# Attention in a two-layer block: outputs moved behind the exponentials, one more buffer, LN(x) in pairs, small tiles shared

## The chip, the core and the metric

The kernel runs on one core of one Trainium2 chip. The core has five engines with a queue of instructions each: TensorE (PE in the profile; PEld are its weight loads), VectorE (DVE), ScalarE (ACT), GpSimd (POOL) and SyncE (SP), and 16 DMA engines that they share. An engine works through its queue in order, and waits where an instruction waits. The metric is the device time of one execution in microseconds (us); lower is better.

## The reference

The input x is 4 images of 32 x 32 tokens with 384 channels, in float32. Two layers follow, each an attention part and a feed-forward part with a residual:

```python
x = x + L0_conv(LN(x))      # attention with 12 heads of 32, described below
x = x + L0_ffn(LN(x))       # 4 experts of width 1536, each token goes to 2 of them
x = x + L1_conv(LN(x))      # outlook attention over 3x3 neighbourhoods
x = x + L1_ffn(LN(x))       # a feed-forward part whose weights are Kronecker products
```

The change lies in the first of these:

```python
attn = softmax(q @ k.T * scale)               # per image and head: 1024 x 1024
gidx = argmax(q @ gp.T)                       # each query goes to one of 48 groups
q_mean = mean of q over each group
tidx = top_k(q_mean @ k.T, 96)                # per group: its 96 best keys
col = number of groups that have chosen a key
attn = attn * (row * col)                     # row is 1 for each query
attn = attn / (attn.sum(axis=queries) + 1e-8) # normalized again, per key
out = (attn @ v) @ proj_w.T
```

## The kernel before

The program runs attention for the four images, then the experts, then the second layer. Everything in the first layer is emitted in an order written out by hand: within `tc.manual_schedule`, the queues of PE, DVE, ACT and SP get their instructions in the order of the Python code (only POOL's are ordered by the framework). What stands earlier in the code runs earlier on its engine.

**Steps.** `attention` has 48 heads (4 images x 12), and each head has 4 steps (`PAIRS`), so 192 steps. Keys lie on the partitions: a step handles two blocks of 128 keys against all 1024 queries. The loop at L838 emits each step in this order:

- `out` (L680), for the step seven earlier (`OUT`): four products of the weighted values `wv` with the two tiles `e` of that step, summed over a head's four steps in the PSUM tile `ps_o`. After a head's last one `keep` (L685) copies `ps_o` to the SBUF tile `po`, and four DMAs put it into the head's rows of `q`: two from SP, then two from POOL that accumulate.
- `scores` (L606): four products of 32 rows each, k times q, into two PSUM tiles `ps_s` of 128 x 1024 (there are two).
- At a head's first step, `gather` (L641) for the head before: ScalarE copies the PSUM sums `z` to `zr`, which go by DMA through a row in DRAM into `zz`.
- `exps` (L619): two `exp` on ScalarE, `ps_s` to two tiles `e`. `ep` has `EBUFS` = 14 of these.
- `spread` (L653), in the second step: adds the halves of `zz` into `zall`, takes reciprocals, and sends them by DMA to all partitions (`rz`).
- Other work: projections of the image before, values, and the units of `prepared` (L785). The generators `groups` and `prepare` yield a unit with its estimated TensorE time and a condition; units are taken while `spent` is below `goal`, which grows by `PACE` = 2.6 us a step.
- `total` (L636): four products of ones with the new tiles `e`, into `ps_z`.
- `share` (L664), for the step six earlier (`SHARE`): VectorE multiplies two tiles `e` by `rz` and the factor `inv`, sums them, and scales the values into `wv`.
- `search` (L795), twice: up to two running searches for the 96 best keys take one turn each, a pass of ScalarE over 128 x 1024 (`Sign` with a sum, written to `junk`, which lies in `below`) or a few small VectorE instructions.

**LN(x).** `prepare` (L442) normalizes an image's eight token tiles one by one: a unit of 0.9 us emits a tile's normalization on ScalarE (`xn`, two buffers), and then the three TensorE transposes and the ScalarE copy of the tile before (`turn`). Several units can fall into one step.

**Small tiles.** `zall` holds the sums of all 48 heads; at the end (L886 to L898) they are checked for their range together with other conditions. The router (`Router.route`, L1255, and after it `first` and `schedule`) sorts tokens to experts, with temporaries named by `temp`; its table is written by 16 indirect DMAs for each image from POOL's queue.

Of the kernel before, what the change touches and what calls it, by code (L numbers as in the profile page):

```python
# [10 lines left out]
FP = mybir.dt.float32  # L11
AF = mybir.ActivationFunctionType
ALU = mybir.AluOpType
AX = mybir.AxisListType
PSUM = bass.MemoryType.PSUM

P = 128
# [21 lines left out]
AHEAD = 3  # L39
EBUFS = 14  # L40
REACH = 2 * IMG + 2
# [112 lines left out]
def attention(net, outer, router, x, x1, unsafe, qkv_wT, gpT, proj_wT, proj_w, gate_w, gate_b):  # L154
# [24 lines left out]
    with ExitStack() as ctx:  # L179
# [72 lines left out]
        junk = below.bitcast(mybir.dt.bfloat16)  # L252
        zall = const.tile([P, NHEAD, NB], FP, name="zall")
        onehot = const.tile([P, B * KC * NB // 2], FP, name="onehot")
# [187 lines left out]
        def prepare(b):  # L442
# [10 lines left out]
            im["mean"] = few.tile([P, NB], FP, name="mean", tag="mean", bufs=3)  # L453
            im["std"] = few.tile([P, NB], FP, name="std", tag="std", bufs=3)
            im["x"] = few.tile([P, NB, NE], FP, name="gate_x", tag="gate_x", bufs=3)

            def turn(xn, o):
                ps = psum()
                for c in range(KC):
                    nc.tensor.transpose(ps[:, c * P : (c + 1) * P], xn[:, c * P : (c + 1) * P], net.ident)  # L460
                nc.scalar.copy(xnT[:, :, o : o + P], ps[:, :C].rearrange("p (c t) -> p c t", c=KC))

            behind = None
            for half in range(2):
                if half and b:
                    yield 0, after(2)
                xt = xts.pop((b, half))
                mv = tiny.tile([P, 4, 2], FP, name="ln_mv", tag="ln_mv", bufs=2)
                rs = tiny.tile([P, 4], FP, name="ln_rs", tag="ln_rs", bufs=2)
                off = tiny.tile([P, 4], FP, name="ln_off", tag="ln_off", bufs=2)  # L470
                for t in range(4):
                    st = tiny.tile([P, 6], FP, name="ln_st", tag="ln_st", bufs=2)
                    nc.vector.bn_stats(st, xt[:, t, :])
                    nc.vector.bn_aggr(mv[:, t, :], st)
                    if t % 2:
                        yield 0.3, None
                std = im["std"][:, 4 * half : 4 * half + 4]
                nc.scalar.activation(std, mv[:, :, 1], AF.Sqrt, bias=net.eps["c"])
                yield 0.3, after(1) if b else None
                nc.vector.tensor_copy(im["mean"][:, 4 * half : 4 * half + 4], mv[:, :, 0])  # L480
                nc.vector.reciprocal(rs, std)
                nc.vector.scalar_tensor_tensor(off, mv[:, :, 0], -1.0, rs, ALU.mult, ALU.mult)
                for t in range(4):
                    yield 0.9, None
                    xn = work.tile([P, C], FP, name="xn", tag="xn")
                    nc.scalar.activation(
                        xn, xt[:, t, :], AF.Identity, bias=off[:, t : t + 1], scale=rs[:, t : t + 1]
                    )
                    if behind is not None:
                        turn(*behind)  # L490
                    behind = xn, (4 * half + t) * P
                if half == 0 and b:
                    fetch(b, 1)
                elif half and b + 1 < B:
                    if b == 0:
                        gating()
                    fetch(b + 1, 0)
            yield 0.9, None
            turn(*behind)
            for c in range(KC):  # L500
# [83 lines left out]
        class Head:  # L584
# [68 lines left out]
            def spread(self):  # L653

                z = zall[:, self.n, :]
                nc.vector.tensor_tensor(z, self.zz[:, 0, :], self.zz[:, 1, :], ALU.add)
                rr = tiny.tile([P, NB], FP, name="rr", tag="rr", bufs=2)
                nc.vector.reciprocal(rr, z)
                there = rows.tile([NTOK], FP, name="r_row", tag="r_row")
                nc.sync.dma_start(out=there.rearrange("(p i) -> p i", i=NB), in_=rr)  # L660
                self.rz = work.tile([P, NTOK], FP, name="rz", tag="rz")
                nc.sync.dma_start(out=self.rz, in_=there.partition_broadcast(P))

            def share(self, u):  # L664
# [20 lines left out]
            def keep(self):  # L685

                po = work.tile([P, 512], FP, name="po", tag="po", bufs=1)
                nc.scalar.copy(po, self.po)
# [30 lines left out]
        def project(b, t):  # L719
            im = images[b]  # L720
            r = b * NTOK + t * P
            if t == 0:
                im["o"] = few.tile([P, NB, NE], FP, name="gate_o", tag="gate_o")
                im["mv"] = few.tile([P, NB, 2], FP, name="mv", tag="mv")
# [21 lines left out]
        def routed(b):  # L746
# [11 lines left out]
            nc.scalar.activation(rs, im["mv"][:, :, 1], AF.Sqrt, bias=net.eps["t"])  # L758
            logit = few.tile(wide, FP, name="logit", tag="logit")
            part = few.tile(wide, FP, name="logit_part", tag="logit_part")  # L760
            mean = im["mean"]
# [76 lines left out]
        for step in range(STEPS + OUT + 2):  # L838
            n, u = divmod(step, PAIRS)
            if 0 <= step - OUT < STEPS:  # L840
                heads[(step - OUT) // PAIRS].out((step - OUT) % PAIRS)
                if (step - OUT) % PAIRS == PAIRS - 1:
                    heads[(step - OUT) // PAIRS].keep()
            if n < NHEAD:
# [3 lines left out]
            if n < NHEAD:  # L848
                heads[n].exps()
            b, i = divmod(step, PAIRS * NH)  # L850
            goal = min(goal + (RAMP if step < 12 else PACE), spent + MOST)
# [33 lines left out]

        good = ep.tile([P, NTOK], FP, name="good", tag="e")[:, : 2 * NHEAD * NB + B * KC * NB // 2 + 2 * B * 5]  # L886
        nz = NHEAD * NB
        flat = zall.rearrange("p n i -> p (n i)")
        nc.vector.tensor_scalar(good[:, :nz], flat, ZMAX, None, ALU.is_le)
        nc.vector.tensor_scalar(good[:, nz : 2 * nz], flat, 1 / ZMAX, None, ALU.is_ge)  # L890
        no = 2 * nz + B * KC * NB // 2
        nc.vector.tensor_scalar(good[:, 2 * nz : no], onehot, 8.0, None, ALU.is_equal)
        nc.vector.tensor_scalar(good[:, no : no + B * 5], topped[:, 0, :], 0.0, None, ALU.is_gt)
# [292 lines left out]
class Router:  # L1186
# [68 lines left out]
    def route(self, b, logit, mean, rs):  # L1255
# [39 lines left out]

        run = [self.temp(f"run_{n}", wide) for n in range(2)]
        src, d = sel, 1
# [32 lines left out]
        yield  # L1330
        ids = self.temp("ids", [P, NB, self.LINE], mybir.dt.int32)
        nc.gpsimd.iota(ids, pattern=[[P, NB], [0, self.LINE]], base=b * NTOK, channel_multiplier=1)
# [13 lines left out]
    def first(self):  # L1346
# [4 lines left out]
        nc.vector.tensor_scalar(full, self.upto[:, B - 1, :], -float(XB), None, ALU.add)  # L1351
        fills = self.temp("fills", shape)
        nc.vector.tensor_tensor(
# [54 lines left out]
    def schedule(self, pool):  # L1408

        nc = self.nc  # L1410
        shape = [P, NE, self.NJ]
        fills = self.temp("fills", shape)
        taken = self.temp("taken", [P, NE])
# [798 lines left out]
```

## Time and profile before

| what | value |
|---|---|
| median of 3 runs | 2989.33 us (2986.28 to 2994.61) |
| the profiled execution | 2999.3 us, span 2997.0 us |
| attention | start to about 1290 us |
| mean granted TensorE clock | 0.97 |
| scores, sums, outputs (L612, L630): instructions each | 1536 |
| one `exp` (L622) | 1109 ns, 384 times |
| one `share` multiplication (L668) | 1272 ns, 384 times |
| one `Sign` pass (L366) | 1149 ns, 160 times |

A line of the profile names the code line, the engine, the operation, and what it writes and reads (`ps_z<-e,rt_ones` is a product of `e` and ones into `ps_z`), then a count. In the waits, a line tells who waited for whom: total, times and the longest. In an order of time, a line has start, length, and in brackets the idle time of the engine before it and what ended it. In a stretch of time, a line has the stretch, its length, and then busy time and instructions of PE, PEld, DVE, ACT and POOL, then the granted TensorE clock, the busy share of the DMA engines and GB/s. Each float32 product shows as two instructions.

### The profile page before, as it was taken

What the parts mean: (1) busy time and instruction counts of PE and PEld (TensorE: products, weight loads), DVE (VectorE), ACT (ScalarE), POOL (GpSimd) and SP (SyncE); (2) the same over time, 40 slices, a digit from 0 to 9 for tenths busy, and PEclk for the clock granted to TensorE, in tenths of its full rate; (3) what the DMA queues carried; (4) which work ended last, traced back from release to release, by engine and by line L of the source; (5) the groups of instructions that cost most, each with busy time, mean ns of one, the idle gap of its engine ahead of it and who ended that gap; (6) DMA issues with size and microseconds to landing.
All of it is one profiled execution on the core that took longest, in us unless ns stands there. A gap on an engine that the chain in (4) does not pass through costs nothing.

```text
span 2997.0 us, 36619 instructions
## 1 busy us (share of the span) xinstructions
PE 2793.7 (93%) x13236; PEld 1509.3 (50%) x13236; DVE 1349.4 (45%) x3703; ACT 1217.0 (41%) x2023; POOL 399.3 (13%) x499
## 2 busy tenths in 40 slices
PE   6979998999899987688999999999999998999988
PEld 4323333333333431156777777777777754444433
DVE  1466676766776677534000001111111137877642
ACT  3777777677777765312111211211211122222125
POOL 1000000200021003113111112222221101100000
PEclk9999999999999998889999999999999999999989
DMA  5133334322322233254445545555555617654432
GB/s 100 46 87 99 92 92 117 81 56 62 96 57 57 65 93 104 69 172 153 182 166 189 190 175 194 213 214 196 206 214 201 232 52 231 197 173 145 161 103 86
DMA packets 216991, 405.90 MB, mean 135 GB/s; under 512 B 83505, under 2 KB 177905, under 8 KB 203745
## 3 DMA queue, kind: packets, MB, share of 16 engines
q1 hardware_dynamic: 186656, 190.77, 21.5%
q0 software_dynamic: 27152, 209.66, 20.4%
q10 hardware_dynamic: 2992, 3.03, 0.3%
q8 instruction: 107, 1.75, 0.3%
q14 instruction: 84, 0.68, 0.1%
HBM read 305.35 MB, written 49.99 MB: 119 GB/s over the span
## 4 chain that ended last, share of the span: by engine, by line
PE 50%; DMA 3%; issue 3%; DVE 3%; ACT 1%; POOL 0%; DVEq 0%; POOLq 0%; ACTq 0%; SPq 0%
PE ps_h L1584 18%; PE ps_y L1601 17%; PE ps_a L1712 4%; PE ps_y L1814 3%; DMA yt<-yg,index 2%; PE ps_wo L1830 1%; PE ps_v L1756 1%; PE ps_h L1984 1%; PE ps_c L1777 1%; PE ps_y L1995 1%; PE ps_t L1541 1%; PE ps_z L630 1%; DMA o<-in_x_dram 1%; PE ps_o L2008 0%; PE ps_o L630 0%
## 5 line engine op out<-in xcount | busy, mean ns | idle before, releaser
L1588 ACT ACTIVATE h<-ps_h,up 128x256 f32<-128x256 f32 x420 | 198.6, 473 | 930.2 <-PE ps_h L1584 930.2
L1584 PE MATMUL ps_h<-xbT,up 128*128 128x256 f32 x2520 | 557.1, 382 | 0.8 <-DVE xbT L1542 0.7
L1601 PE MATMUL ps_y<-down,h 128*128 128x384 f32 x1680 | 556.9, 489 | 0.0
L1584 PEld LDWEIGHTS ps_h<-xbT,up 128*128 128x128 f32 x2520 | 482.7, 192 | 77.0 <-DVE xbT L1542 1.1
L668 DVE CUSTOM_DVE_ANT_0 e<-e,rz,inv 128x1024 f32<-128x1024 f32 x384 | 474.2, 1272 | 59.5 <-DMA rz<-r_row 59.3
L622 ACT ACTIVATE e<-ps_s,shift 128x1024 f32<-128x1024 f32 x384 | 406.5, 1109 | 199.6 <-PE ps_s L612 199.2
L1601 PEld LDWEIGHTS ps_y<-down,h 128*128 128x128 f32 x1680 | 318.5, 191 | 208.2 <-issue 3.5
L1606 DVE TENSOR_TENSOR y<-ps_y,down 128x384 f32<-128x384 f32 x70 | 39.0, 558 | 729.6 <-PE ps_y L1601 729.6
L630 PE MATMUL ps_z<-e,rt_ones 128*32 128x512 f32 x1536 | 297.4, 636 | 63.1 <-ACT e L622 63.1
L630 PE MATMUL ps_o<-e,wv 128*32 128x512 f32 x1536 | 277.6, 644 | 25.7 <-DVE wv L675 15.0
L612 PE MATMUL ps_s<-q,k 32*128 32x512 f32 x1536 | 224.1, 654 | 0.0
L695 POOL DMA_DIRECT2D q<-po x96 | 75.7, 876 | 1063.1 <-DMA q<-po 547.1
L366 ACT ACTIVATE below<-tk_left,tk_bound 128x1024 bf16<-128x1024 f32 (+1 forms) x160 | 183.9, 1149 | 11.3 <-DVE tk_bound L372 7.0
L1712 PE MATMUL ps_a<-wa,xnT 128*128 128x486 f32 x384 | 167.2, 584 | 8.1 <-DVE attn L1722 6.3
L630 PEld LDWEIGHTS ps_z<-e,rt_ones 128*32 128x32 f32 x1536 | 45.7, 109 | 228.3 <-ACT e L622 190.1
L612 PEld LDWEIGHTS ps_s<-q,k 32*128 32x128 f32 x1536 | 61.4, 187 | 173.8 <-issue 139.4
L630 PEld LDWEIGHTS ps_o<-e,wv 128*32 128x32 f32 x1536 | 66.8, 115 | 150.5 <-issue 110.5
L281 PE MATMUL ps_t<-xnT,wqkv 128*128 128x512 f32 x288 | 138.6, 623 | 2.8 <-ACT tk_left L325 1.8
L1712 PEld LDWEIGHTS ps_a<-wa,xnT 128*128 128x128 f32 x384 | 71.7, 192 | 92.6 <-issue 86.2
L1553 DVE SCALAR_TENSOR_TENSOR x<-yt,weight,x 128x384 f32<-128x384 f32 x38 | 23.5, 618 | 191.4 <-DMA x<-x 190.7
L1814 PE MATMUL ps_y<-band,v 128*32 128x194 f32 (+2 forms) x960 | 102.7, 517 | 6.9 <-DMA band<-room 6.6
L1467 POOL DMA_INDIRECT yt<-yg,index x64 | 65.8, 1028 | 289.2 <-DVE x L1553 142.4
(338 smaller groups left out, 2865.5 us busy)
## 6 DMA issues: line engine op xcount, KB each, us to landing
band<-room SPq DMA_DIRECT2D x32, 1560.0 KB
rz<-r_row SPq DMA_DIRECT2D x48, 512.0 KB
yg<-y SPq DMA_DIRECT2D x70, 192.0 KB
q<-q SPq DMA_DIRECT2D x192, 64.0 KB
k<-k SPq DMA_DIRECT2D x192, 64.0 KB
room<-none SPq DMA_DIRECT2D x64, 192.0 KB
x<-x SPq DMA_DIRECT2D x38, 192.0 KB
o<-in_x_dram SPq DMA_DIRECT2D x33, 192.0 KB
```

Of the source, the lines that this page charges most:

```text
L281: nc.tensor.matmul(ps, lhsT=lhsT(k), rhs=rhs(k), start=k == 0, stop=k == KC - 1)
L366: nc.scalar.activation(junk[:n], left[:n], AF.Sign, bias=bound[:n], accum_out=over[:n])
L612: nc.tensor.matmul(ps[:, half * 512 : half * 512 + 512], lhsT=self.k4[r, u * P : (u + 1) * P], rhs=self.q4[r, :], start=True, stop=True,)
L622: nc.scalar.activation(e, ps, AF.Exp, bias=shift, scale=QK_SCALE)
L630: nc.tensor.matmul(ps[r : r + 32, :], lhsT=lhsT(odd), rhs=self.es[2 * u + odd][:, half * 512 : half * 512 + 512], start=u == 0, stop=u == ...
L668: nc.vector.tensor_tensor_reduce(self.es[m], self.es[m], self.rz, 1.0, self.im["inv"][:, m, self.h : self.h + 1], ALU.mult, ALU.add, self. ...
L695: nc.gpsimd.dma_start(out=there, in_=po[r : r + 32, :], accum_op=ALU.add)
L1584: nc.tensor.matmul(ps, lhsT=up[:, o : o + P], rhs=xbT[:, k, :], start=k == 0, stop=k == KC - 1,)
L1588: nc.scalar.activation(h, ps, AF.Gelu, bias=up[:, KC * HID + f : KC * HID + f + 1])
L1601: nc.tensor.matmul(ps, lhsT=hs[f][:, t * P : (t + 1) * P], rhs=down[:, f * C : (f + 1) * C], start=f == 0, stop=f == NF - 1,)
L1712: nc.tensor.matmul(pa[:, hh, :HW_], lhsT=xnT[:, k, :], rhs=wa[:, k, hh * HW_ : (hh + 1) * HW_], start=k == 0, stop=k == KC - 1,)
L1814: nc.tensor.matmul(ys[c][32 * n : 32 * n + 32, lo - 512 * half : hi - 512 * half], lhsT=vs[b, t][:, h * HD : (h + 1) * HD], rhs=bands[b, t ...
```

## The change

It moves `out` and `keep` in each step from before `scores` to behind `exps`, and gives `ep` 15 tiles. `prepare` works on pairs of tiles: a unit of 1.8 us first transposes and copies the pair that the unit before normalized, then emits the normalizations of the next pair; for images 1 to 3 a unit waits for the step after. `po` gets the buffer of `zr`. `zall` becomes a tile for each image, whose range check is made when the image's last head comes to `spread`, with `below` for scratch, into `fit`. `gate_o`, `logit` and `logit_part` get one buffer instead of two, and in the router `run_0`, `run_1`, `ids` and `fills` get the buffers `run`, `prob`, `ge` and `gt`.

```diff
-EBUFS = 14
+EBUFS = 15
...
+            im["z"] = tiny.tile([P, NH, NB], FP, name="zall", tag="zall", bufs=2)
...
-            behind = None
+            behind = []
...
-                for t in range(4):
-                    yield 0.9, None
-                    xn = work.tile([P, C], FP, name="xn", tag="xn")
-                    nc.scalar.activation(
-                        xn, xt[:, t, :], AF.Identity, bias=off[:, t : t + 1], scale=rs[:, t : t + 1]
-                    )
-                    if behind is not None:
-                        turn(*behind)
-                    behind = xn, (4 * half + t) * P
+                for two in range(2):
+
+                    yield 1.8, after(1) if b else None
+                    while behind:
+                        turn(*behind.pop(0))
+                    for t in (2 * two, 2 * two + 1):
+                        xn = work.tile([P, C], FP, name="xn", tag="xn")
+                        nc.scalar.activation(
+                            xn, xt[:, t, :], AF.Identity, bias=off[:, t : t + 1], scale=rs[:, t : t + 1]
+                        )
+                        behind.append((xn, (4 * half + t) * P))
...
-            yield 0.9, None
-            turn(*behind)
+            yield 1.8, after(1) if b else None
+            while behind:
+                turn(*behind.pop(0))
...
-                z = zall[:, self.n, :]
+                z = self.im["z"][:, self.h, :]
...
+                if self.h == NH - 1:
+                    every = self.im["z"].rearrange("p h i -> p (h i)")
+                    n = NH * NB
+                    nc.vector.tensor_scalar(below[:, :n], every, ZMAX, None, ALU.is_le)
+                    nc.vector.tensor_scalar(below[:, n : 2 * n], every, 1 / ZMAX, None, ALU.is_ge)
+                    nc.vector.tensor_reduce(fit[:, self.b : self.b + 1], below[:, : 2 * n], AX.X, ALU.min)
...
-                po = work.tile([P, 512], FP, name="po", tag="po", bufs=1)
+                po = work.tile([P, 512], FP, name="po", tag="zr", bufs=1)
...
-                im["o"] = few.tile([P, NB, NE], FP, name="gate_o", tag="gate_o")
+                im["o"] = few.tile([P, NB, NE], FP, name="gate_o", tag="gate_o", bufs=1)
...
-            logit = few.tile(wide, FP, name="logit", tag="logit")
-            part = few.tile(wide, FP, name="logit_part", tag="logit_part")
+            logit = few.tile(wide, FP, name="logit", tag="logit", bufs=1)
+            part = few.tile(wide, FP, name="logit_part", tag="logit_part", bufs=1)
...
-            if 0 <= step - OUT < STEPS:
-                heads[(step - OUT) // PAIRS].out((step - OUT) % PAIRS)
-                if (step - OUT) % PAIRS == PAIRS - 1:
-                    heads[(step - OUT) // PAIRS].keep()
             if n < NHEAD:
                 heads[n].scores(u)
             if u == 0 and 0 < n <= NHEAD:
                 heads[n - 1].gather()
             if n < NHEAD:
                 heads[n].exps()
+            if 0 <= step - OUT < STEPS:
+                heads[(step - OUT) // PAIRS].out((step - OUT) % PAIRS)
+                if (step - OUT) % PAIRS == PAIRS - 1:
+                    heads[(step - OUT) // PAIRS].keep()
...
-        run = [self.temp(f"run_{n}", wide) for n in range(2)]
+        run = [self.temp(n, wide) for n in ("run", "prob")]
...
-        ids = self.temp("ids", [P, NB, self.LINE], mybir.dt.int32)
+        ids = self.temp("ge", [P, NB, self.LINE], mybir.dt.int32)
...
-        fills = self.temp("fills", shape)
+        fills = self.temp("gt", shape)
```

More of the change, by code (lines that the diff above doesn't have):

```diff
@@ L252, in attention @@
         junk = below.bitcast(mybir.dt.bfloat16)
-        zall = const.tile([P, NHEAD, NB], FP, name="zall")
+        fit = const.tile([P, B], FP, name="fit")
         onehot = const.tile([P, B * KC * NB // 2], FP, name="onehot")
@@ L884, in attention @@
         assert pending == [None, None] and begun == len(tiles) and not searching and not zeros
[L886 to L892, printed above, removed]
+        good = ep.tile([P, NTOK], FP, name="good", tag="e")[:, : B + B * KC * NB // 2 + 2 * B * 5]
+        nc.vector.tensor_copy(good[:, :B], fit)
+        no = B + B * KC * NB // 2
+        nc.vector.tensor_scalar(good[:, B:no], onehot, 8.0, None, ALU.is_equal)
         nc.vector.tensor_scalar(good[:, no : no + B * 5], topped[:, 0, :], 0.0, None, ALU.is_gt)
@@ L1411, in schedule @@
         shape = [P, NE, self.NJ]
-        fills = self.temp("fills", shape)
+        fills = self.temp("gt", shape)
         taken = self.temp("taken", [P, NE])
```

## The prediction

> **What bounds the kernel now.** The profiled execution took 2999.3 us around a span of 2997.0; the runs' median, 2989.33, lies 10 us below it. I sum savings against the profiled execution and subtract them from the median. A measurement of this kernel tells about 0.3% (9 us) from no change.
>
> I read first the page's busy times, then the stretches in time. The change works from the start to about 1290 us, where attention ends; behind it TensorE is 100% busy with the experts in most slices, in the program's order, so time saved in attention is saved at the end.
>
> ```profile
> PE 2793.7 (93%) x13236; PEld 1509.3 (50%) x13236; DVE 1349.4 (45%) x3703; ACT 1217.0 (41%) x2023; POOL 399.3 (13%) x499
> ```
> ```profile
> 60.00:1170.00 1110.00, 1014.39 (x5717) 383.01 (x5720) 743.39 (x2186) 793.16 (x1205) 109.74 (x125) 0.96 0.30 76
> ```
> In attention TensorE is 91% busy, ScalarE 71%, VectorE 67%: TensorE has 96 us of idle time. The waits of that stretch say on what:
>
> ```profile
> ACT e L622 <- PE ps_s L612: 169.2, 149, 3.9
> ...
> PE ps_z L630 <- ACT e L622: 44.6, 50, 3.2
> ...
> PE ps_t L460 <- ACT xn L486: 25.8, 11, 4.3
> ```
> The sums wait for exponentials (44.6 us), the transposes for LN(x) (25.8). ScalarE's 169.2 us is a circle: exponentials wait for scores, scores stand in TensorE's queue behind the outputs, which stand behind the sums, which wait for the exponentials before. TensorE's own order in time (start, length) shows that circle binding:
>
> ```profile
> 1171.82 1.14 PE L612 MATMUL ps_s<-q,k 32*128 32x512 f32 x8
> 1174.19 1.63 PE L630 MATMUL ps_z<-e,rt_ones 128*32 128x512 f32 x6 [1.23 <-ACT e L622]
> ...
> 1177.03 1.14 PE L612 MATMUL ps_s<-q,k 32*128 32x512 f32 x8
> ```
> Scores to scores is 5.21 us: 2.37 to the first sum (ScalarE begins 1.17 after the scores, one exponential ends 1.06 later), then 2.84 for the rest of the sums, which wait for the second exponential, and the outputs. A step with enough other work is bound by TensorE instead:
>
> ```profile
> 351.12 1.06 PE L630 MATMUL ps_z<-e,rt_ones 128*32 128x512 f32 x8
> 352.00 1.04 PE L630 MATMUL ps_o<-e,wv 128*32 128x512 f32 x8
> 352.97 1.14 PE L612 MATMUL ps_s<-q,k 32*128 32x512 f32 x8
> 354.05 2.84 PE L281 MATMUL ps_t<-xnT,wqkv 128*128 128x512 f32 x6
> 356.82 1.07 PE L630 MATMUL ps_z<-e,rt_ones 128*32 128x512 f32 x8
> ```
> From start to start: sums 0.88, outputs 0.97, scores 1.07, work 2.77; 2.92 plus the work.
>
> I sorted steps 7 to 190 by these distances: 46 of 5.2 us with the sums under 2.4 after the scores (circle, little other work); 35 of 5.2 with the sums 2.9 to 3.2 after (circle and TensorE about level); 61 bound by TensorE (mean 6.54); 13 with LN transposes (mean 8.25); 29 mixed, waiting for VectorE or for a late ScalarE (mean 7.18).
>
> **The change part by part. 1, outputs between scores and sums.** The first steps, before any outputs exist, show what remains of the circle:
>
> ```profile
> 90.97 2.06 PE L630 MATMUL ps_z<-e,rt_ones 128*32 128x512 f32 x8 [0.36 <-ACT e L622]
> 92.95 1.14 PE L612 MATMUL ps_s<-q,k 32*128 32x512 f32 x8
> ...
> 97.66 1.06 PE L630 MATMUL ps_z<-e,rt_ones 128*32 128x512 f32 x8
> 98.66 1.14 PE L612 MATMUL ps_s<-q,k 32*128 32x512 f32 x8
> ```
> Sums that wait for their exponentials to scores: 1.98. So the new circle is 2.34 + 1.98 = 4.33 (rounded up), against 5.19. The outputs fit inside: 1.07 + 0.97 = 2.04 after the scores, before the 2.34. For the 46 steps I take the larger of 4.33 and ScalarE's load (2.2 for the exponentials plus its other work in that step): −34 us. In the 35 level steps TensorE's work is 4.8 to 5.1 already; with ScalarE's load the same rule gives +5.
>
> The **rule against it**: the Trainium skill, "TensorEngine Tiling (Array Packing)", Key Properties, says that changing the tiling mode drains TensorE. Sums and outputs use 128x32 tiles, scores 32x128, other work the whole array. Today a step switches three times, since outputs follow sums in one mode; afterwards four times. The row: sums to outputs 0.88, sums to scores without a wait 1.00, so 0.12 for a switch. Scores to outputs does not occur in this trace; like scores to other work it would be 1.07. Outputs to other work occurs nowhere either: 0.97 to 1.07. The sum becomes 3.04 to 3.14 instead of 2.92. I take +0.17, between the ends: 61 steps, +10 us. By the rule without a price one could fear a full drain of some 0.5 us (a scores instruction lasts 0.59 beyond the last start at 0.55): +30.
>
> In the 29 mixed steps an output waits for VectorE's wv. Today scores and exponentials queue behind it; afterwards they are already done when it comes. An isolated delay then gains up to 2 us; in a row of them VectorE's own 3.3 us a step (2 x 1.27, 0.17, 0.23, reads) remains. I take −12, ends 0 and −25.
>
> **2, 15 buffers.** With outputs behind the exponentials, 16 tiles would be live; with 15 the second exponential waits for the first half of the same step's outputs. These start 1.07 after the scores and take 1.0; the second exponential would start at 2.23 anyway. Zero, covered by 0.2 us; where wv is late the exponential is late too, as today.
>
> **3, LN in pairs.** Today up to three tiles fall into a step and go round: normalize (0.71), transpose, copy (0.47), each waiting for the other:
>
> ```profile
> 475.22 1.87 PE L460 MATMUL ps_t<-ident,xn 128*128 128x128 f32 x6 [2.35 <-ACT xn L486]
> ```
> The 13 steps take 107 us; their TensorE work is 13 x 2.92 plus 33.5 (24 tiles at 0.66, five blocks of L281, some small), 71.5: 36 us lost, part of it to the clock (0.81 granted in the stretch 471 to 480). Afterwards images 1 to 3 use 15 steps of two tiles, whose transposes find xn ready. ScalarE then sets the step: 2.2 + 2 x 0.71 + 2 x 0.47 + about 1.3 searches of 1.35 = 6.3. That is 95 us, and some 8 for the work pushed to other steps, against 107 plus two ordinary steps, 118: −15; with less clock lost −18. At the start, image 0 loses: a pair goes transposes, copies, two normalizations in series, some 1 us more a pair for three pairs: +3.
>
> **4, shared tiles.** `po` takes `zr`'s single buffer. So the copy of z (L644), which stands before the exponentials in ScalarE's queue, must wait until all four DMAs of the previous `po` have read it; the last two accumulate from POOL's queue. For 43 heads I compared the end of the `po` copy, the last landing (2.6 us after issue, by its row) and the next copy of z. Today there are 3.9 us to spare in the median. But `keep` moves behind the exponentials, so `po` is copied 3.15 us later; SP's queue, where the head's eight q and k loads stand before it, often hides part of that, leaving 1.5 us in the median, negative for six heads (worst −3.0). The pace takes 0.9 more for two steps, and 0.65 is covered because the exponentials wait for scores anyway. Sum over those heads: +13. One head is worse: POOL is full with the table's scatters and expert weights:
>
> ```profile
> 1202.88 0.95 POOL L1522 DMA_INDIRECT xb<-x,ids  x1 [6.92 <-DMA ids<-table,rows_t_first]
> 1205.62 1.82 POOL L695 DMA_DIRECT2D q<-po  x2
> ```
> Its `po` was copied at 1182.34, the next z at 1191.85: the new wait would reach to about 1210, with the exponentials, the searches and then the sums behind it. But this place stalls today as well (steps 181 and 182 take 10.7 and 10.9 while z and its reciprocals travel), so I count +7, not 18. `fit` adds three VectorE instructions of some 0.2 us for each of four images, in its slack (else +2), and takes 384-wide ones off the end: −1. `ids` in `ge`'s buffer waits for reads over three steps old; one-buffer `gate_o` and `logit` come again 48 steps later: zero, hidden behind those distances; without them a few us at most.
>
> Sum: −34 + 5 + 10 − 12 − 18 + 3 + 20 − 1 = −27. The profiled execution would take 2972; the median **2962 us**. Its own range, from the ends above with half of each, is 2945 to 2980.
>
> **The rivals.** *Everything lands in time* (0.24): the shared buffer costs 5 instead of 20, late outputs give 20, LN 25; the saving is 57: 2932. For it: landings are estimated, and SP waits hide much of the 3.15; against: six heads are over already. *The gain goes to ScalarE and the drain* (0.13): a drain of 0.4 costs 24 instead of 10, and other engines hold a third of the 46 circle steps (−22 instead of −34): +26 on −27, so 2988. For it: ScalarE is loaded over 2.1 us beside its exponentials in 48 of the 61 TensorE-bound steps; against: the 0.12 row. *Slower* (0.11): the shared buffer stalls every head. Without its 20 the change saves 47; over 47 heads a mean stall of 1.0 us takes all of it, 1.2 makes it measurably slower; at 1.5 the time is 3013. For it: accumulating DMAs landed up to 6.8 us after issue in this trace; against: a stall in one step lengthens the distance for the next head.
>
> **How the numbers follow.** My forecast has 0.52. Faster: 0.52 + 0.24 = 0.76; same 0.13; slower 0.11. The range reaches from the second case's far side, 2915, to 2996, above the no-change case and short of the slower one.
>
> **What would show it.** Right: many steps of 4.3 to 4.4; sums' wait for exponentials below 15 us; transposes' wait for xn near zero; scores to outputs near 1.07; a new wait of zr for the DMA of po, mainly near 1200 us. Wrong: steps of 5.2 that stay, zr waiting at every head, or outputs starting over 1.4 after the scores.

## The result, and the profile after

The changed kernel takes 2966.94 us (median of 4 runs, 2966.79 to 2967.68), the kernel before 2988.86 (4 runs beside it, 2986.28 to 2994.61): a ratio of 0.992, 95% interval 0.9903 to 0.9937, or 22 us less. The forecast was 2962, its own range 2945 to 2980. The profiled execution of the changed kernel took 2966.8 us around a span of 2964.9, so here profile and median agree, while the profile of before stood 10 us above its median.

The page's busy times of the changed kernel, its stretch from 60 to 1150 us, and below it the same stretch of the kernel before:

```profile
PE 2780.2 (94%) x13236; PEld 1472.9 (50%) x13236; DVE 1349.2 (46%) x3714; ACT 1213.7 (41%) x2023; POOL 395.1 (13%) x499
```
```profile
60.00:1150.00 1090.00, 1014.85 (x5779) 353.75 (x5779) 751.27 (x2217) 797.50 (x1215) 113.80 (x133) 0.97 0.30 78
```
```profile
60.00:1150.00 1090.00, 999.76 (x5649) 378.58 (x5648) 729.84 (x2123) 783.89 (x1194) 102.99 (x118) 0.97 0.30 77
```
The work is the same (13236 TensorE instructions in both); within the same 1090 us TensorE now runs 5779 of them instead of 5649. The last scores of attention start at 1223.7 instead of 1260.9 us (-37), the experts start 31.8 us behind them instead of 31.3, and the rest of the program takes 1709.3 us instead of 1704.9. That rest is no cost of the change that a single trace could show: in a second trace of the changed kernel it took 1703.1. The two profiled executions differ by 32 us and the medians by 22, so some of the 37 belongs to the slower execution that was profiled before.

TensorE's waits of the changed kernel in that stretch (engine, what waits, its releaser: sum, times, longest), and below them ScalarE's largest:

```profile
PE ps_z L634 <- ACT e L626: 45.5, 37, 4.5
PE ps_o L634 <- DVE tk_parts L370: 10.1, 6, 4.1
PE ps_t L281 <- ACT xnT L462: 5.1, 2, 3.6
PE ps_t L461 <- DVE g L549: 3.4, 1, 3.4
PE ps_t L461 <- DVE gate_o L746: 2.6, 2, 2.1
```
```profile
ACT e L626 <- PE ps_s L616: 77.3, 95, 3.1
```
The exponentials' wait for scores, the sign of the circle, fell from 169.2 (in the slightly longer stretch shown of before) to 77.3. The transposes no longer wait for `xn` (25.8 before). But the sums' wait for exponentials, which I expected below 15, is 45.5, as large as before (44.6), and the transposes have found other things to wait for.

TensorE's order in time, first in a step that TensorE bounds (start, length):

```profile
342.09 1.06 PE L634 MATMUL ps_z<-e,rt_ones 128*32 128x512 f32 x8
343.08 1.14 PE L616 MATMUL ps_s<-q,k 32*128 32x512 f32 x8
344.15 1.07 PE L634 MATMUL ps_o<-e,wv 128*32 128x512 f32 x8
345.15 2.84 PE L281 MATMUL ps_t<-xnT,wqkv 128*128 128x512 f32 x6
347.92 1.06 PE L634 MATMUL ps_z<-e,rt_ones 128*32 128x512 f32 x8
```
From start to start: sums 0.99, scores 1.07, outputs 1.00, work 2.77. Without the work that is 3.06, against 2.92 before. And a step with little other work:

```profile
1192.76 1.14 PE L616 MATMUL ps_s<-q,k 32*128 32x512 f32 x8
1193.83 1.06 PE L634 MATMUL ps_o<-e,wv 128*32 128x512 f32 x8
1195.13 2.06 PE L634 MATMUL ps_z<-e,rt_ones 128*32 128x512 f32 x8 [0.23 <-ACT e L626]
1197.12 1.14 PE L616 MATMUL ps_s<-q,k 32*128 32x512 f32 x8
1198.19 1.06 PE L634 MATMUL ps_o<-e,wv 128*32 128x512 f32 x8
```
Scores to scores is 4.36 here (4.33 in most such steps), where it was 5.21. The outputs lie inside what used to be waiting.

One step is new and bad, step 180, 20.5 us long. TensorE:

```profile
1158.82 1.06 PE L634 MATMUL ps_o<-e,wv 128*32 128x512 f32 x8
1175.42 2.93 PE L634 MATMUL ps_z<-e,rt_ones 128*32 128x512 f32 x8 [15.53 <-ACT e L626]
```
ScalarE at the same time:

```profile
1173.77 0.58 ACT L648 COPY zr<-ps_z 128x512 f32<-128x512 f32 x1 [17.05 <-DMA q<-po]
```
and POOL, whose queue holds the two accumulating DMAs that `zr` waits for:

```profile
1156.70 1.13 POOL L1508 DMA_INDIRECT up<-in_wup_dram,rows_w_first  x1 [0.30 <-issue]
1158.13 2.79 POOL L1508 DMA_INDIRECT down<-in_wdown_dram,rows_w_first  x1 [0.30 <-issue]
1161.22 0.95 POOL L1519 DMA_INDIRECT ids<-table,rows_t_first  x1 [0.31 <-issue]
1162.17 1.81 POOL L705 DMA_DIRECT2D q<-po  x2
```
`po` was copied at 1151.65. Its DMAs on POOL came out only at 1162.17, behind scatters of the table and the first expert's weights, and the second landed only at 1173.6, 10.8 us after its issue at 1162.78, while those weights moved. Behind the copy of z stood the exponentials, behind them the sums. The steps 181 and 182, which stalled before (10.7 and 10.9 us), take 5.1 each, so this stall is mostly the old one in another place: step 180 takes 15.3 us more, these two 11.4 less.

### The profile page after: what moved, and what is told of

The parts are those of the page before. It is cut to its first block, busy times and chain, and to the rows that moved or that the text cites. A ratio compares the mean times of both kernels' runs of the same rounds, so it can differ in the third digit from the quotient of the medians.

```text
span 2964.9 us, 36625 instructions
## 1 busy us (share of the span) xinstructions
PE 2780.2 (94%) x13236; PEld 1472.9 (50%) x13236; DVE 1349.2 (46%) x3714; ACT 1213.7 (41%) x2023; POOL 395.1 (13%) x499
## 3 DMA queue, kind: packets, MB, share of 16 engines
q10 hardware_dynamic: 2992, 3.03, 0.3%
## 5 line engine op out<-in xcount | busy, mean ns | idle before, releaser
L634 PE MATMUL ps_z<-e,rt_ones 128*32 128x512 f32 x1536 | 276.4, 625 | 64.9 <-ACT e L626 64.9
L634 PE MATMUL ps_o<-e,wv 128*32 128x512 f32 x1536 | 214.2, 629 | 24.2 <-DVE wv L685 14.1
L366 ACT ACTIVATE below<-tk_left,tk_bound 128x1024 bf16<-128x1024 f32 (+1 forms) x160 | 184.0, 1150 | 39.0 <-DVE col L431 15.8
L616 PEld LDWEIGHTS ps_s<-q,k 32*128 32x128 f32 x1536 | 62.2, 190 | 169.2 <-issue 169.2
L281 PE MATMUL ps_t<-xnT,wqkv 128*128 128x512 f32 x288 | 137.4, 618 | 6.8 <-ACT xnT L462 5.1
L634 PEld LDWEIGHTS ps_o<-e,wv 128*32 128x32 f32 x1536 | 31.1, 109 | 180.3 <-issue 69.4
```

Of the source, the lines that this page charges most:

```text
L281: nc.tensor.matmul(ps, lhsT=lhsT(k), rhs=rhs(k), start=k == 0, stop=k == KC - 1)
L366: nc.scalar.activation(junk[:n], left[:n], AF.Sign, bias=bound[:n], accum_out=over[:n])
L616: nc.tensor.matmul(ps[:, half * 512 : half * 512 + 512], lhsT=self.k4[r, u * P : (u + 1) * P], rhs=self.q4[r, :], start=True, stop=True,)
L634: nc.tensor.matmul(ps[r : r + 32, :], lhsT=lhsT(odd), rhs=self.es[2 * u + odd][:, half * 512 : half * 512 + 512], start=u == 0, stop=u == ...
```

## The experiments

All kernels of a group ran on one chip beside the kernel before. The chips were not equally fast: the kernel before took 2989 us beside the first group, 3020 beside the second, 2991 beside the third and 3010 beside the last run, so across groups only ratios are compared. Where lines are shorter, line numbers shift by a few: scores 613 to 616, exponentials 623 to 626, sums and outputs 631 to 634.

### First group: the parts taken back one at a time

**The old order, with everything else as changed.**

```diff
         for step in range(STEPS + OUT + 2):
             n, u = divmod(step, PAIRS)
+            if 0 <= step - OUT < STEPS:
+                heads[(step - OUT) // PAIRS].out((step - OUT) % PAIRS)
+                if (step - OUT) % PAIRS == PAIRS - 1:
+                    heads[(step - OUT) // PAIRS].keep()
             if n < NHEAD:
                 heads[n].scores(u)
...
                 heads[n].exps()
-            if 0 <= step - OUT < STEPS:
-                heads[(step - OUT) // PAIRS].out((step - OUT) % PAIRS)
-                if (step - OUT) % PAIRS == PAIRS - 1:
-                    heads[(step - OUT) // PAIRS].keep()
```

> The changed kernel with out and keep in front of scores again, everything else (15 buffers, pairs, shared tiles) as changed. Theory (the circle from scores to scores falls from 5.2 to 4.3 us and TensorE-bound steps pay 0.14 for one more switch of mode): steps of 5.2 come back, some 80 of them, and 0.14 per TensorE-bound step is saved; 2980 to 2992. Rival (the saving is that of the LN pairs alone): 2963 to 2970.

Measured: 3000.98 us (2996.82 to 3009.26), ratio 1.0038 (1.0024 to 1.0052), slower than the 2980 to 2992 that I expected. The order is worth 34 us, and all the other edits together cost 12. The waits from 60 to 1260 us of this kernel:

```profile
ACT e L626 <- PE ps_s L616: 177.1, 150, 4.0
...
PE ps_z L634 <- ACT e L626: 91.0, 67, 19.4
```
The circle is back. All 191 steps of this kernel hold the same other TensorE work as those of the changed one, so the two traces can be compared step by step, from step 7 on:

| steps, sorted by the old order | count | old order, us | changed, us | difference |
|---|---|---|---|---|
| circle (5.15 to 5.25, sums under 2.45 after the scores) | 39 | 202.7 | 179.7 | -23.0 |
| level (5.15 to 5.25, sums later) | 34 | 176.5 | 176.7 | +0.2 |
| with LN transposes | 12 | 83.8 | 82.3 | -1.5 |
| all others but step 180 | 98 | 653.3 | 641.6 | -11.7 |
| step 180 | 1 | 25.1 | 20.5 | -4.6 |

The rows add up to 41 us, not 34: the execution of the old order that was profiled was the slowest of its five, 8 us above their median, so up to 7 us of the rows can belong to that execution.

27 of the 39 circle steps now take 4.33 to 4.36; the others have something else in ScalarE's queue. Among the 98 others are some 40 that TensorE bounds; each is longer by 0.14, nearly the same in all of them. The mixed steps there gain the more: single ones 1 to 2.4 us, steps 126 and 174 5.8 each, of which 4.2 and 4.8 come back in 127 and 175.

**14 buffers instead of 15, everything else as changed.**

```diff
-EBUFS = 15
+EBUFS = 14
```

> The changed kernel with 14 buffers of exponentials. Theory (with 16 tiles live, 15 make only the second exponential wait, which costs nothing; 14 make the first wait for the same step's outputs as well, which start 1.07 us after the scores and last 1.0): the circle is 2.1 + 1.1 + 1.98 = 5.2 us again, and TensorE-bound steps stay; 2985 to 2995. Rival (the buffer is not needed, TensorE has other work to cover it): 2966 to 2972.

Measured: 3022.36 us (3019.98 to 3028.0), ratio 1.0118 (1.0101 to 1.0135): 55 us slower than the changed kernel and 33 slower than before. ScalarE's largest wait from 60 to 1260 us, and TensorE's order in a step with little other work:

```profile
ACT e L626 <- PE ps_o L634: 227.6, 152, 4.3
```
```profile
1245.35 1.14 PE L616 MATMUL ps_s<-q,k 32*128 32x512 f32 x8
1246.42 1.07 PE L634 MATMUL ps_o<-e,wv 128*32 128x512 f32 x8
1248.69 2.06 PE L634 MATMUL ps_z<-e,rt_ones 128*32 128x512 f32 x8 [1.20 <-ACT e L626]
1250.68 1.14 PE L616 MATMUL ps_s<-q,k 32*128 32x512 f32 x8
```
The first exponential now waits for outputs of the same step to leave its buffer. It starts 2.17 after the scores instead of 1.17, and scores to scores is 5.33: just 1.00 more than with 15. No step of this kernel from the seventh on is under 5.25; 111 of them lie between 5.25 and 6. The new order with one buffer too few is worse than the old order. I had expected at most half of this loss (2985 to 2995). Step by step against the changed kernel, the 33 steps that took under 4.4 us pay most of it, 1.1 each and 36.5 in all; 53 of 4.4 to 5.3 pay 0.33 on the mean, 17.7; the 98 longer ones pay nothing in sum. With 15 buffers the exponentials of the same stretch hardly wait for outputs:

```profile
ACT e L626 <- PE ps_o L634: 2.4, 4, 0.7
```

**LN(x) tiles one by one, everything else as changed.**

```diff
-                for two in range(2):
-
-                    yield 1.8, after(1) if b else None
-                    while behind:
-                        turn(*behind.pop(0))
-                    for t in (2 * two, 2 * two + 1):
-                        xn = work.tile([P, C], FP, name="xn", tag="xn")
...
+                for t in range(4):
+                    yield 0.9, None
+                    xn = work.tile([P, C], FP, name="xn", tag="xn")
...
+                    if behind is not None:
+                        turn(*behind)
+                    behind = xn, (4 * half + t) * P
```

> The changed kernel with LN tiles one by one, each transposed behind the next normalization, as before the change. Theory (pairs take out the round trip between ScalarE and TensorE, 15 to 18 us for images 1 to 3): 2980 to 2986, and the transposes wait some 20 us or more for xn. Rival (with outputs between scores and sums the transposes find their xn anyway): 2965 to 2971.

Measured: 2963.91 us (2956.32 to 2967.31), ratio 0.992 (0.9903 to 0.9937): the same as the changed kernel, and far from the 2980 to 2986 of my theory. And yet the wait that the pairs remove is there again (60 to 1150 us):

```profile
PE ps_z L631 <- ACT e L623: 31.9, 31, 3.4
PE ps_t L461 <- ACT xn L487: 26.8, 12, 4.7
PE ps_o L631 <- DVE tk_parts L370: 5.0, 3, 3.4
```
What the pairs save in one wait (26.8), others take back: the sums' wait for exponentials is 13.6 smaller without pairs, that for `tk_parts` 5.1. All waits of TensorE in this stretch together are 73.7 us here and 75.2 in the changed kernel. TensorE is busy 1016.2 of the 1090 us here and 1014.9 in the changed kernel. In stretches of steps, with the number of TensorE instructions other than scores, sums and outputs:

| steps | one by one, us (instructions) | pairs, us (instructions) | difference |
|---|---|---|---|
| 12 to 23 (LN of image 1) | 79.1 (98) | 76.7 (86) | -2.4 |
| 24 to 47 | 129.4 (188) | 134.9 (200) | +5.5 |
| 60 to 75 (LN of image 2) | 105.4 (124) | 98.9 (118) | -6.5 |
| 76 to 95 | 117.8 (184) | 119.3 (190) | +1.5 |
| 108 to 123 (LN of image 3) | 101.8 (130) | 96.0 (116) | -5.8 |
| 124 to 143 | 119.8 (180) | 127.2 (192) | +7.4 |
| 144 to 155 | 67.0 (116) | 69.4 (118) | +2.4 |

The pairs do make the LN stretches 14.7 us shorter. But they also push 32 instructions of other work into the steps behind, which take 16.8 longer. At 0.47 us an instruction (2.84 for six at L281) 32 of them are 15.0 us. The sums of the three LN stretches, one by one and then in pairs (length, then busy time by engine), show what the 14.7 are:

```profile
sum 286.30, PE 253.33 PEld 83.67 DVE 199.34 ACT 215.24 POOL 17.33; mean PE 84.44 PEld 27.89 DVE 66.45 ACT 71.75 POOL 5.78
```
```profile
sum 271.61, PE 243.11 PEld 78.78 DVE 196.92 ACT 211.88 POOL 17.06; mean PE 81.04 PEld 26.26 DVE 65.64 ACT 70.63 POOL 5.69
```
10.2 us of them are TensorE's busy time, work that left the stretch; its idle time fell only from 33.0 to 28.5, although the wait for `xn` is gone. In the four stretches behind, its busy time rises by 14.5 us and its idle time by 2.3. So the pairs removed a wait, but hardly any idle time. (The execution profiled one by one was the fastest of its four, 8 us below their median. A second pair of traces, the two kernels with late weights below, shows the same in the LN stretches: 13.0 us shorter, 8.5 of it busy time.)

**`po` in a buffer of its own.** For the memory, the copy of z goes into the head's own `rz` tile instead.

```diff
-                zr = work.tile([P, 512], FP, name="zr", tag="zr", bufs=1)
+                self.rz = work.tile([P, NTOK], FP, name="rz", tag="rz")
+                zr = self.rz[:, :512]
...
-                self.rz = work.tile([P, NTOK], FP, name="rz", tag="rz")
...
-                po = work.tile([P, 512], FP, name="po", tag="zr", bufs=1)
+                po = work.tile([P, 512], FP, name="po", tag="po", bufs=1)
```

> The changed kernel, but po has a buffer of its own; zr takes the first half of the head's rz tile, so that the memory stays the same. Theory (the copy of z waits for the accumulating DMAs of po): no wait of zr for the DMA of po is left, the 20.5 us step near 1160 us falls, but z's own transfer then meets the expert weights as it did before the change, so some 5 to 10 us of stall stay; 2967 becomes 2950 to 2960. Rival (the stall near 1160 us is the loading of the expert weights, and sharing the buffer is harmless): 2964 to 2970.

Measured: 2966.84 us (2965.71 to 2968.47), ratio 0.9928 (0.9911 to 0.9944): no change, as the rival said. ScalarE's waits from 1150 to 1200 us have no entry of `zr` for a DMA any more, but

```profile
ACT e L626 <- PE ps_s L616: 13.7, 6, 6.1
ACT e L626 <- PE ps_o L634: 9.9, 1, 9.9
```
VectorE shows what is late instead:

```profile
1172.94 0.17 DVE L661 TENSOR_TENSOR zall<-zz 128x8 f32<-128x8 f32 x1 [11.08 <-DMA zz<-z_row]
...
1181.25 1.28 DVE L678 CUSTOM_DVE_ANT_0 e<-e,rz,inv 128x1024 f32<-128x1024 f32 x1 [4.94 <-DMA rz<-r_row]
```
z gets out in time, its 8 KB are read back by a DMA issued at 1163.11, and this is then 10 us on its way, while the weights are. The stall stands in step 182 (17.8 us) instead of 180 (20.5). So the sharing was not its only cause. (In this trace the experts do start 4.9 us earlier than in the changed kernel's, at 1250.6; the medians do not show it.)

### Second group: two edits alone, and the weights moved

**The pairs alone, on the kernel before** (the part of the diff from `behind = []` to the second `turn`, nothing else).

> The kernel before with only the LN(x) tiles in pairs, transposed a step behind. The step of the prediction (-18 for images 1 to 3, +3 at the start): 2974. Rival (the steps with LN get shorter, and the work that they pushed aside and other waits take it back): 2986 to 2992, with the transposes' wait for xn gone and the sum of all waits of TensorE as before.

Measured: 3020.64 us against 3019.82, ratio 1.0003 (0.9986 to 1.0021). No gain with the old order either, as the rival said. Beside the next kernel, which has the tiles one by one and ran on the same chip, steps 12 to 23 take 71.1 us instead of 82.3, steps 24 to 47 142.9 instead of 138.0. In the three LN stretches together TensorE's idle time is 33.8 us instead of 38.0.

**The sharing alone, on the kernel before.**

```diff
-                po = work.tile([P, 512], FP, name="po", tag="po", bufs=1)
+                po = work.tile([P, 512], FP, name="po", tag="zr", bufs=1)
```

> The kernel before with only po in the buffer of zr; the outputs stay ahead of the scores, so po is copied some 3 us earlier than in the changed kernel. Theory (sharing costs only at the one head that meets the expert weights, and there it displaces a later stall): 2987 to 2997. The step of the prediction (13 over the heads and 7 at one, less the 3 us of later copies): 2995 to 3005. If the 12 us by which the old order with all other edits is slower than the kernel before are all of the sharing: 3001.

Measured: 3028.09 against 3019.82, ratio 1.002 (1.0009 to 1.003), 6 us slower by the ratio (8 by the medians). On the chips of the first group that would be some 2995, where the two expectations meet. But the trace decides for the first, in that only one head waits, at step 180:

```profile
ACT zr L644 <- DMA q<-po: 5.9, 1, 5.9
```
The 6 us are half of the 12 us of the old order's experiment; the other half is not separated (the other shared tiles, `fit`, the 15th buffer under the old order, or the interval's width).

**The first expert's weights held back** in the changed kernel. A copy of their row numbers onto themselves makes the loads wait for this step:

```diff
             begin(step)
+            if step == 189:
+                nc.vector.tensor_copy(router.firsts[0], router.firsts[0])
             if step < 12:
```

> The changed kernel with one VectorE instruction more: at step 189 the row numbers of the first experts' weights are copied onto themselves, so that the loads of the first expert's weights, which POOL issued at 1157 us, between the end of one head's outputs and the travel of its sums, are issued only after about 1200. Theory (the weights hold up whatever a head sends in those 12 us, the shared buffer is only the first to meet them): the wait of 15.5 us of the sums at step 180 falls below 3, nothing takes its place, time 2952 to 2956. Rival (it is the shared buffer itself that waits for the accumulating DMAs): the wait of zr for po stays over 10 us, time 2964 to 2969. Rival (the first expert now waits for its weights): attention ends 12 us earlier, but the first expert's matrix products start no earlier, time 2964 to 2970.

Measured: 2996.78 against 3019.82, ratio 0.9927 (0.9898 to 0.9957): no gain. The weights now left POOL at 1241 us and met the last head. TensorE's order there:

```profile
1268.53 1.94 PE L634 MATMUL ps_o<-e,wv 128*32 128x512 f32 x8 [12.02 <-DVE wv L685]
...
1287.07 5.49 PE L1593 MATMUL ps_h<-xbT,up 128*128 128x256 f32 x12 [0.65 <-DVE xbT L1551]
```
The wait before the last head's outputs was 5.76 and is 12.02; the experts start 39.0 us behind the last scores instead of 31.8. At step 180 `zr` still waits, 8.2 us: `po` was copied at 1186.21, but POOL issued its part only at 1195.13, behind six small gathers that now stand first in its program; they landed within 3.7 us, not 11.5 as in the changed kernel. So two things made the wait of the changed kernel, a place far back in POOL's queue and the traffic; moving the weights took only the second away, and made the last head pay for it. The time is that of the two rivals, but neither's wait was seen: `zr` waited less than 10 us, and the first expert's products waited for their tokens 0.65 us, as in the changed kernel. What waited was the last head.

**The same, with LN one by one.**

> The same late weights, and the LN(x) tiles normalized and transposed one by one as before. Theory (LN in pairs gains nothing, its idle time reappears elsewhere): within 4 us of the kernel with late weights and pairs, 2949 to 2956. Rival (the pairs' 18 us were hidden by the stall at step 180, which ran longer in the pairs' kernel for other reasons): 2965 to 2972.

Measured: 2992.73 against 3019.82, ratio 0.9902 (0.9876 to 0.9927), 4 us below the kernel with pairs in the same group, with intervals that overlap: again nothing from the pairs.

### Third group: a gap for the weights

**The changed kernel again**, to compare with on the same chip.

> The changed kernel itself, so that the other kernels of this call can be laid beside it on the same chip. If the gain does not depend on the chip, a ratio of 0.992 to the kernel before (0.990 to 0.994).

Measured: 2967.02 (2963.75 to 2981.05), ratio 0.9926 (0.99 to 0.9951).

**The weights at step 186, or at step 182, each with `po` in its own buffer.**

```diff
-            if step == 189:
+            if step == 186:
```
(and 182), with the edit of `po` shown above.

> The changed kernel with po in a buffer of its own and the first expert's weights held back to step 186, behind the loads of q and k of the last head and ahead of the last two heads' travels. Theory (a head waits if its transfers meet the weights or stand behind POOL's gathers, and only then; with both taken away and the weights in a gap, nothing waits): steps 175 to 190 together, 97 us in the changed kernel, fall to 78 to 86, the experts start 31 to 33 us after the last scores, the time is 10 to 18 us below the changed kernel's on the same chip. Rival (the gap is too short, the weights meet the travel of the last head but one as at step 189): within 4 us of the changed kernel.

> The same with the weights held back only to step 182, just behind the travel of one head's sums, so that they meet the loads of q and k of a head that starts two steps later. Theory: if these loads land in time nevertheless, 10 to 18 us below the changed kernel on the same chip; if the weights hold them up, the scores of step 184 wait for q or k by up to 8 us, and the gain is 2 to 8 us. Rival (the place does not matter): within 4 us of the kernel with the weights at step 186.

Measured: at 186, 2967.95 (2960.54 to 2971.86), ratio 0.9913 (0.989 to 0.9936), no clear gain; at 182, 2960.52 (2959.83 to 2961.61), ratio 0.9892 (0.9876 to 0.9909), 6.5 us below the changed kernel. Neither reaches the 10 to 18 us of the theory. Steps 175 to 190 take 93.3 and 87.9 us; 96.9 in the changed kernel of this group. TensorE's waits from 1150 to 1260 us at 186:

```profile
PE ps_o L634 <- DVE wv L685: 12.2, 5, 6.4
PE ps_s L616 <- DMA k<-k: 6.5, 2, 6.3
```
at 182:

```profile
PE ps_o L634 <- DVE wv L685: 16.3, 8, 5.0
PE ps_z L634 <- ACT e L626: 6.2, 12, 1.6
```
and in the changed kernel of this group:

```profile
PE ps_z L634 <- ACT e L626: 21.3, 14, 15.8
PE ps_o L634 <- DVE wv L685: 12.7, 6, 5.6
```
The waits for `wv` behind the last scores are in all three; in the changed kernel they are the whole 12.7, at 186 the whole 12.2, at 182 all but 4.4. So at 186 the scores of the last head wait for `k`, 6.3 us, in place of the 15.8. At 182 only two waits for `wv` are new, 4.0 and 0.4 us in steps 186 and 187; the scores of step 184, which I had named, do not wait. The place does matter, and none of the three places tried is free.

**The weights at step 182, `po` alone, and LN one by one.**

> The first weights held back to step 182, po in a buffer of its own, and the LN(x) tiles one by one as before. Theory (pairs bring nothing, and cost some 3 us where their work is pushed into the steps behind): a ratio of 0.986 to 0.989 to the kernel before, some 2957 on a chip where that takes 2990, and steps 12 to 47 together about 3 us shorter than with pairs (208 to 209 against 211 to 212). Rival (the pairs do bring something that the stall covered): a ratio over 0.991.

Measured: 2970.18 against 3010.2, ratio 0.9859 (0.9832 to 0.9887), the lowest of all ratios; on the chips of the first group that would be some 2947. My expectation for steps 12 to 47 was missed: they took 214.8, not 208 to 209, with one step of 11.2 in them that no other kernel with tiles one by one shows under the new order. It ran on a slower chip than the kernel with pairs, so the 3 thousandths between the two rest on ratios whose intervals overlap slightly. That it is faster than the changed kernel (0.990 to 0.9951) is plain from the intervals; how much of that is from the LN tiles is not.

## Why the prediction was right, and where its steps were not

**The time** (2962 against 2966.94) and the sign came out, and the largest step is confirmed alone.

**Outputs between scores and sums**: my sum was -34 + 5 + 10 - 12 = -31; taking the order back costs 34. The new circle of 4.33 is exact. Its steps were fewer than the 46 I counted (27 reach it, 39 belong to it), so it gave 23 instead of 34; the level steps gave nothing instead of losing 5; the rest makes up for it, with 12 won over all other steps although some 40 of them pay for the switch. Up to 7 us of these rows can belong to the one slow execution, so the sum is better shown than its terms.

**The rule against it**: the additional change of tiling mode exists and is small. The row that I took (0.12) was the right guide: scores to outputs 1.07, outputs to other work 1.00, in sum 0.14 for a step where I took 0.17. A drain of 0.4 us, the rival's price, or of 0.5 is excluded: no TensorE-bound step shows it.

**15 buffers at zero** was right, and nearer to the edge than the text says: "covered by 0.2 us" is true of the second exponential (2.4 us of waits in all), and with one buffer less the first one waits as well, which costs 1.00 in a circle step and 55 us in all. The 15th buffer is no part with a value of its own; it is what makes the order possible, and the shared tiles are what make room for it.

**LN in pairs**, -18 + 3, is the step that failed; measured are 0 (alone), and 3 to 4 in favour of one by one (twice, each within the intervals). The round trips did vanish: no transpose waits for `xn`. But I took the LN steps' idle time for time to be won, 23 us before the pushed work and 26 with the clock, and in the three stretches only 4.5 us of idle time went under the new order; the other 10.2 of the 14.7 are work that left. The second term that was mis-sized is "some 8 for the work pushed to other steps": it is 17, because TensorE has little idle time where this work lands. Where the idle time went is shown: 13.6 of the 26.8 us came back as the sums' wait for exponentials, 5.1 as the outputs' for `tk_parts`, the rest as waits of transposes and projections for other tiles (`xnT` 5.1, `g` 3.4, `gate_o` 2.6), so that all waits are 75.2 us with pairs and 73.7 without. Which engine's order made them take over was not tested. The +3 at the start does not show: the first scores start between 80.7 and 82.0 us in all traces, with pairs and without.

**Shared `po`**: +20 on paper; alone, under the old order, it measured +6, and in the changed kernel nothing (2966.84 without it). The profile does show the wait near 1200 us that I named, 17.05 us against some 18, and no other over 3 us: the 13 over the other heads were an overestimate, since two other waits of 3.5 us together are all that came of them. The 7 for the one head, counted net of the stalls behind it, is about 4. On this term the rival in which everything lands in time, with its 5, was nearer than my forecast.

**The signs I named**: many steps of 4.3 to 4.4, outputs 1.07 after scores, `xn` near zero and one wait of `zr` near 1200 us, all seen. The sums' wait below 15 us was wrong (45.5). In steps of under 5.3 us it did fall, from 21.6 to 6.7 us (60 to 1150 us), but in longer steps it rose from 21 to 39, the longest in single steps with a late ScalarE (4.5 in step 173, 4.1 in 171), and 13.6 of it is what LN's lost wait turned into.

The two errors, LN 15 too good and sharing some 15 to 20 too bad, nearly cancelled; that is luck. All edits but the order were forecast at +4 together and measured +12 under the old order, of which the pairs are 0, sharing 6, and 6 stay open. That the total came out within 5 us is owed to this as well as to the order's term.

## What to carry to other kernels

A wait that vanishes at one place is worth only the idle time that goes with it: compare the bound engine's idle time, not the length of the stretch, count the instructions that leave the stretch, and price them where they land, at full length if that place is bound by the same engine. When work is reordered inside a ring of buffers, count the live buffers at the moment of each write: one too few turned 22 us gained into 33 lost. And a large load that is issued early can have a price wherever it lands (here at all places tried): look which small, urgent transfers share those microseconds, and in which queue they stand behind it, before blaming the buffer that waits for them.

## What the runs showed of the hardware that I had not expected

The price of a changed tiling mode is nearly constant: 0.14 us for a step with one more of them, in 38 of some 40 TensorE-bound steps (0.10 to 0.12 in the others).

Small transfers fare badly beside gathers of weights. The changed kernel's stretch from 1155 to 1176 us (its last two numbers are the DMA engines' busy share and GB/s):

```profile
1155.00:1176.00 21.00, 4.70 (x26) 0.94 (x28) 7.72 (x25) 3.95 (x5) 12.43 (x12) 0.68 0.66 248
```
That is 66% at 248 GB/s, against 30% and 78 GB/s on the mean of the attention stretch. In that time an accumulating DMA on POOL's queue took 10.8 us to land (2.4 in the median of the profile), and in the kernel with its own `po` an 8 KB read on SP's queue took 10 us as well. So it is not POOL's queue alone that is slow. Why such transfers are held up, no run here shows.

On the chip of the second group the profiles show single steps 5 to 12 us longer than on the first, near steps 82, 129 and 177, while the table is scattered; for several of their waits the profile shows no releaser. In the changed kernel with late weights three such steps (81, 129, 177) are 29 us longer than in the changed kernel on the first chip, about what the kernel before takes longer on this chip (31). What it is stays open.
